# The last tile of a Winograd convolution in joint stages, and the place of a bound's product

## The chip, the cores and the metric

The kernel runs on one core of a Trainium2 chip. Its time is the device time of one launch in microseconds (us); lower is better. The core's engines are TensorE (PE; its weight loads are listed as PEld), VectorE (DVE), ScalarE (ACT), GpSimd (POOL) and SyncE (SP), which issues DMA transfers. Each engine works through its own instructions in order and waits on semaphores for the others.

## The reference

The input `x` is (4, 256, 48, 48) in float32. Two layers are applied, each to a group norm of `x` and with a residual.

```python
# layer 0
h = relu(batch_norm(conv3x3(gn(x))))                 # 256 -> 256 channels
q, k, v = split(qkv_w @ h + qkv_b)                   # 8 heads of 32
a = softmax(q^T k * 32 ** -0.5)
x = x + proj_w @ (v a^T) + proj_b
# layer 1
g = conv3x3(gn(x))                                   # 45 channels
outs = [gn(x)]
for i, d in enumerate((1, 6, 12, 24, 36)):
    w = softmax(g[:, 9 * i : 9 * i + 9])             # nine weights per pixel
    outs.append(sum of nine shifts of gn(x) by -d, 0, d, each times its weight)
y = conv1x1(concat(outs))
x = x + batch_norm(y)
```

## The kernel before

Channels lie on the 128 partitions in NH = 2 halves, pixels in the free dimension. The four images pass through two kinds of work: `attention` (layer 0's scores, exponentials and weighing), and the rest. From the second image on, the rest is done in three joint stages: `dynamic_filters` of image b - 1 (layer 1), and in the gaps of it `conv_qkv` of image b (conv, then q's, k's and v's products). The stages run at about 525 to 806, 1186 to 1469 and 1848 to 2107 us of the profiled span; each ends in the attention of image b. Image 0 has `conv_qkv` alone, to 150 us.

**The order of work.** Python writes one order of instructions for each engine. In a joint stage `drive` decides it. It holds several generators ("streams": `loads`, `far`, `rest`, `near`, `filters`, `mixes`) and one filler, `other`, which is `conv_qkv`. Each stream yields a due time; the first stream in the list that is due at the planner's time of TensorE goes next, and only if none is due the filler goes, when `need[0]()` is no later than that time. Otherwise the planner's TensorE time is moved to the soonest due time. The times are kept by `Clock`, one number per engine, raised by fixed prices (480 ns for a VectorE sum out of PSUM, 450 for a ScalarE copy and so on). They decide the order alone; the hardware then runs each engine's list in order.

`either` gives a sum of two SBUF tiles to VectorE or GpSimd, whichever the clocks say ends sooner (900 against 1300 ns for 576 elements, half of that for 288). `busy_dve` tells whether VectorE's clock is over 500 ns ahead of both ScalarE's and TensorE's.

**The conv in joint stages, `conv_blocks`.** It is a Winograd convolution in rows and columns. `Blocks` makes the transformed inputs (`stage0`, `rest`, `along`); the transformed weights are fetched by `taken`, two tiles ahead. There are twelve tiles, `TILES`: a row index i out of ORDER = (1, 2, 3, 4, 0, 5) and an output half o. A tile has four products, for the column indices j = 1, 2, 0, 3 (n = 0 to 3), each over the two input halves, into a PSUM tile of 128 x 288 out of a pool with two banks (tag "c", `psum_tile`; `free["c"]` and `slot("c", 2)` keep the planner's times of release). The column transform back is

- n = 0: ScalarE copies the product into `one` (L1190);
- n = 1: with a busy VectorE, ScalarE copies into `two[:, 1]` (L1195), and two `either` sums make `two[:, 0]` = one + product and `two[:, 1]` = one - product; else VectorE does both from PSUM (L1200, L1201);
- n = 2, 3: product + `two[:, 0]`, or `two[:, 1]` - product, into every second column of `y`: with a busy VectorE a ScalarE copy (L1206) and an `either` sum, else one VectorE sum out of PSUM (L1211, L1213).

The row transform back is in `before`, called within the first product, and `after`, called behind the fourth. For i = 1 to 4, `after` makes the sums and differences s12, d12, s34, d34 in `blocks.held`. For i = 5, `before` makes `t` = d12 - 2 d34, the result of row 1, and overwrites d12 with d12 - 8 d34, both by `axpy` on VectorE (L1073); `after` adds d12 to `y`, 576 elements, by `either` (L1102 on GpSimd, L1104 on VectorE), which is row 3. i = 0 goes likewise with rows 2 and 0. A finished row is put on a list by `relu`, and `relus(limit)` issues the ScalarE activations (L1125) that write the conv's output `hid`.

After the last tile, (5, 1), all open relus are issued, and the first product of q (L1255) is open to `drive` from their end on: `need[0]` holds `last[0]`.

**q, k and v, in `conv_qkv`.** q and k are made per chunk of 384 pixels: two products over the halves (L1255), a ScalarE activation that adds the bias (L1262), a VectorE maximum of the absolute values (L1267). v is made in nine steps, t = 0, 2, ..., 16, of two 128-pixel blocks each (L1277), copied by ScalarE to `vT` (L1284). Behind the first, VectorE makes `top` out of the maxima (L1288 to L1290). Behind the ninth, one product of 128 x 2 (L1293) and a VectorE copy (L1294) write `bound`, a bound of the scores, read at the kernel's end:

```python
            pb = psum_tile(f"pb_{b}")
            nc.tensor.matmul(pb[:, :NH], hmat, top[:, 0], start=True, stop=True)
            nc.vector.tensor_copy(bound[:, b, :], pb[:, :NH])
```

`psum_tile` is the same pool of two banks. In image 0 another small product of that pool follows (L2463), and then, as in the other images, the score products (L1331), whose PSUM tiles take over the banks of the pools before.

In the profile, `cv_k`, `cv_q` and `cv_v` are the tiles that hold transformed inputs, `y` and `held`; `pc` is the conv's PSUM tile, `pq` and `pv` those of q, k and of v, `pb` that of the bound. `prod` and `near` (L1828, L1834), `wb` (L1815), `far` (L1762, L1504, L1506), `amat` (L1736), `bmat` (L1724) and `py` (L1926, L1992) belong to the filters' streams.

Of the kernel before, what the change touches and what calls it, by code (L numbers as in the profile page):

```python
# [8 lines left out]
F32 = mybir.dt.float32  # L9
F32R = mybir.dt.float32r  # L10
AF = mybir.ActivationFunctionType
ALU = mybir.AluOpType
# [5 lines left out]
P = 128  # L18
NH = C // P
# [38 lines left out]
def conv_preact_kernel(  # L58
# [12 lines left out]
    nc = tc.nc  # L71
# [463 lines left out]
    hmat = const.tile([P, P], F32, tag="hmat", name="hmat")  # L535
# [5 lines left out]
    bound = const.tile([P, B, NH], F32, tag="bound", name="bound")  # L541
# [10 lines left out]
    with tc.tile_pool(name="w", bufs=1) as wpool, tc.tile_pool(  # L552
        name="act", bufs=1
# [59 lines left out]
        one = wpool.tile([P, 1], F32, tag="one", name="one")  # L613
# [20 lines left out]
        for j in range(2):  # L634
            t = act.tile([P, NH, PADW * PADW], F32, tag=f"pad{j}", name=f"pad{j}")
            t = t.rearrange("p h (r w) -> p h r w", w=PADW)
# [104 lines left out]
        clock = Clock()  # L741
        free = {}

        def slot(tag, bufs):

            ends = free.setdefault(tag, [])
            return ends[-bufs] if len(ends) >= bufs else 0.0
# [14 lines left out]
        XN = 2 * TJ * XT  # L762
        TILES = [(i, o) for i in ORDER for o in range(NH)]
# [334 lines left out]
        def either(out, a, c, op, *after):  # L1098

            part = 0.5 if len(out.shape) == 2 and out.shape[-1] == XN else 1.0  # L1100
            if clock.t["POOL"] + 1300 * part <= clock.alone(*after) + 900 * part:
                nc.gpsimd.tensor_tensor(out, a, c, op)  # L1102
                return clock("POOL", 1300 * part, *after)
            nc.vector.tensor_tensor(out, a, c, op)  # L1104
            return clock.both(900 * part, *after)

        def conv_blocks(b, psum_tile, blocks, pool, hid):

            axpy = blocks.axpy
            tt = nc.vector.tensor_tensor  # L1110
            rows = hid.rearrange("p h (t r w) -> p h t r w", r=4, w=WW)
            spare = list(blocks.spare)

            results, last = [], [0.0]

            def busy_dve():
                return clock.t["DVE"] > max(clock.t["ACT"], clock.t["PE"]) + 500

            def relu(o, r, y, end):
                results.append((o, r, y, end))  # L1120

            def relus(limit):
                while results and results[0][3] + 150 <= limit:
                    o, r, y, end = results.pop(0)
                    nc.scalar.activation(  # L1125
                        rows[:, o, :, r, :], rows_of(y), AF.Relu,
                        bias=bn_t[:, o : o + 1], scale=bn_s12[:, o : o + 1],
                    )
                    clock("ACT", 660, end)

            def before(i, o):

                s12, d12, s34, d34 = (blocks.held[:, j, o] for j in range(4))
                if i == 0:
                    t = spare.pop(0)
                    axpy(t, s34, -4.0, s12)
                    relu(o, 2, t, clock.both(800))
                    either(s12, s12, s34, ALU.subtract)
                elif i == 5:
                    t = spare.pop(0)  # L1140
                    axpy(t, d34, -2.0, d12)
                    relu(o, 1, t, clock.both(800))
                    axpy(d12, d34, -8.0, d12)
                    clock.both(800)

            def target(i, o):

                if i in (1, 3):
                    return blocks.first[o]
                if i in (2, 4):  # L1150
                    return blocks.held[:, 1 if i == 2 else 3, o]
                return spare.pop(0)

            def after(i, o, y):

                s12, d12, s34, d34 = (blocks.held[:, j, o] for j in range(4))
                if i in (2, 4):
                    s, d = (s12, d12) if i == 2 else (s34, d34)
                    either(s, y, blocks.first[o], ALU.add)
                    either(d, blocks.first[o], y, ALU.subtract)  # L1160
                elif i in (0, 5):
                    relu(o, i and 3, y, either(y, y, s12 if i == 0 else d12, ALU.add))

            blocks.scaled()
            need[0] = lambda: 150 + max(slot("c", 2), blocks.end[STEPS[0]])
            for t, (i, o) in enumerate(TILES):
                u = us.pop(t)
                y = target(i, o).rearrange("p (n s) -> p n s", s=2)
                for n, j in enumerate((1, 2, 0, 3)):
                    m = psum_tile(f"pc_{b}_{i}_{o}_{j}")[:, :XN]  # L1170
                    clock("PE", 0, slot("c", 2), blocks.end[i, j])
                    z = blocks.of[i].rearrange("p (j h n) -> p j h n", j=4, h=NH)[:, j]
                    relus(max(clock.t["ACT"], clock.t["PE"]))
                    for h in range(NH):
                        nc.tensor.matmul(
                            m, u[:, h, j], z[:, h], start=(h == 0), stop=(h == NH - 1)
                        )
                        clock("PE", MM * XN / CH)
                        if h == 0:
                            need[0] = lambda: 0.0  # L1180
                            if n == 0:
                                if t + 2 < len(TILES):
                                    us[t + 2] = taken(t + 2)
                                if t == 0:
                                    blocks.along(ORDER[1])
                                before(i, o)
                            yield MM * XN / CH
                    if n == 0:
                        one = pool.tile([P, XN], F32, tag="one", name=f"one_{b}_{i}_{o}")
                        nc.scalar.copy(one, m)  # L1190
                        end = clock("ACT", 400, clock.t["PE"])
                    elif n == 1:
                        two = pool.tile([P, 2, XN], F32, tag="two", name=f"two_{b}_{i}_{o}")
                        if busy_dve():
                            nc.scalar.copy(two[:, 1], m)  # L1195
                            end = clock("ACT", 400, clock.t["PE"])
                            either(two[:, 0], one, two[:, 1], ALU.add, end)
                            either(two[:, 1], one, two[:, 1], ALU.subtract, end)
                        else:
                            tt(two[:, 0], m, one, ALU.add)  # L1200
                            tt(two[:, 1], one, m, ALU.subtract)  # L1201
                            end = clock("DVE", 900, clock.t["PE"], end)
                    else:
                        to = y[:, :, n - 2]
                        if busy_dve():
                            nc.scalar.mul(to, m, 1.0 if j == 0 else -1.0)  # L1206
                            end = clock("ACT", 450, clock.t["PE"])
                            either(to, to, two[:, n - 2], ALU.add, end)
                        else:
                            if j == 0:  # L1210
                                tt(to, m, two[:, 0], ALU.add)  # L1211
                            else:
                                tt(to, two[:, 1], m, ALU.subtract)  # L1213
                            end = clock("DVE", 480, clock.t["PE"])
                        if n == 3:
                            after(i, o, y.rearrange("p n s -> p (n s)"))
                    free["c"].append(end)
                    then = STEPS[4 * t + n + 1] if 4 * t + n + 1 < len(STEPS) else None
                    need[0] = lambda: 150 + max(
                        slot("c", 2), blocks.end.get(then, NEVER) if then else last[0],  # L1220
                    )
                    if n == 3 and o == NH - 1:
                        blocks.passed.add(i)
                    if then is None:
                        relus(NEVER)
                        last[0] = clock.t["ACT"]
                    yield MM * XN / CH
# [4 lines left out]
        def conv_qkv(b, gn, psum_tile, weights, ready, pool, between=()):  # L1232
# [14 lines left out]
            top = small.tile([P, 2, NH], F32, tag="qktop", name=f"qktop_{b}")  # L1247
# [25 lines left out]
            for t in range(0, NT, 2):  # L1273
# [15 lines left out]
                    nc.vector.tensor_tensor(top[:, 0], top[:, 0], top[:, 1], ALU.mult)  # L1289
                    nc.vector.tensor_scalar(top[:, 0], top[:, 0], QS, None, ALU.mult)  # L1290
                yield 4 * MM * C / CH
            pb = psum_tile(f"pb_{b}")
            nc.tensor.matmul(pb[:, :NH], hmat, top[:, 0], start=True, stop=True)  # L1293
            nc.vector.tensor_copy(bound[:, b, :], pb[:, :NH])  # L1294

        qkv = {}
        CONV_QKV = MM * (6 * 4 * 6 * TN / CH + NCK * NH * 4 + NT * 2 * C / CH)
# [1354 lines left out]
```

## Time and profile before

| | us |
|---|---|
| median of three runs | 2724.35 |
| the runs | 2721.27, 2724.35, 2724.39 |
| profiled execution, its own time | 2722.09 |
| its span, first to last instruction | 2720.2 |

| engine | busy us | share of the span |
|---|---|---|
| TensorE, products | 2607.0 | 96% |
| TensorE, weight loads | 1102.1 | 41% |
| VectorE | 2082.2 | 77% |
| ScalarE | 1806.3 | 66% |
| GpSimd | 809.3 | 30% |

A busy share is a mean over stages of different kinds, so a change in one stage is read from that stage: which engine waits there, and for whom. The mean granted clock of TensorE is 0.989 of full speed, and a window of the trace can be asked for its own. In a timeline row the numbers are the start in the span and the length in us, then the engine, the line, the operation, the tiles and shapes, the count, and in brackets how long the engine stood idle before it and what ended that. Products in float32 show as two instructions each.

### The profile page before, as it was taken

Reading aid. Unit: us, or ns where it says so; the run is one execution under the profiler, and the core shown is the slowest. Engines: PE = TensorE matmul, PEld = TensorE weight load, DVE = VectorE, ACT = ScalarE, POOL = GpSimd, SP = SyncE. Lnnn points to the kernel's source line nnn. Section 1 sums busy time; section 2 is a strip of 40 time slices with the busy share of each in tenths; the row PEclk is TensorE's granted clock in tenths of the full one; section 3 lists DMA queues with packets and bytes.
Section 4 is the critical chain, followed back from the end, with each engine's and each line's share of the span. In section 5 each row is a group of like instructions: output and inputs, shape, how many; then the busy total and the mean of one; then the engine's idle time right before and its main releaser. Section 6 shows DMA issues by size and latency. Waiting matters only on the chain. (4 is left out here: it accounts for less than half of the span.)

```text
span 2720.2 us, 42536 instructions
## 1 busy us (share of the span) xinstructions
PE 2607.0 (96%) x16938; PEld 1102.1 (41%) x16938; DVE 2082.2 (77%) x2029; ACT 1806.3 (66%) x2287; POOL 809.3 (30%) x885
## 2 busy tenths in 40 slices
PE   6999999999999999999999999999989999999996
PEld 5632222555562222355555222245546222235554
DVE  7768888757739898857774988885775888885676
ACT  4479888734449898854445888884444888875344
POOL 5200100477520010067750000007775000100453
PEclk9999999999999999999999999999999999999998
DMA  4805445323252445423324354452324444432456
GB/s 174 223 13 105 108 98 110 90 60 108 65 104 58 99 95 108 99 74 87 94 63 84 76 105 99 94 111 75 84 73 120 107 100 99 99 88 72 121 165 219
DMA packets 136942, 273.67 MB, mean 101 GB/s; under 512 B 58024, under 2 KB 98384, under 8 KB 135712
## 3 DMA queue, kind: packets, MB, share of 16 engines
q0 software_dynamic: 26256, 137.71, 22.1%
q1 hardware_dynamic: 110480, 133.17, 18.3%
q8 instruction: 135, 2.21, 0.3%
q14 instruction: 71, 0.58, 0.1%
HBM read 112.12 MB, written 36.04 MB: 54 GB/s over the span
## 5 line engine op out<-in xcount | busy, mean ns | idle before, releaser
L1380 DVE TENSOR_TENSOR acc<-acc,p 128x2048 f32<-128x2048 f32 (+1 forms) x568 | 1052.0, 1852 | 121.0 <-ACT p L1340 71.6
L1340 ACT ACTIVATE p<-se 128x1536 f32<-128x1536 f32 x648 | 938.7, 1449 | 0.0
L1331 PE MATMUL so<-q,k 32*128 32x512 f32 (+1 forms) x1440 | 729.1, 594 | 18.5 <-ACT p L1339 15.9
L1331 PE MATMUL se<-q,k 32*128 32x512 f32 (+1 forms) x4320 | 737.8, 594 | 0.0
L1365 PE MATMUL num<-p,vT 128*32 128x512 f32 (+1 forms) x5760 | 711.9, 561 | 2.2 <-ACT ao L1390 2.2
L1339 ACT ACTIVATE p<-so 128x512 f32<-128x512 f32 x648 | 388.4, 599 | 195.2 <-PE se L1331 89.0
L1331 PEld LDWEIGHTS so<-q,k 32*128 32x128 f32 x1440 | 216.7, 183 | 535.6 <-ACT p L1339 492.0
L1834 POOL TENSOR_TENSOR near<-near,prod 128x384 f32<-128x384 f32 x352 | 353.3, 1037 | 255.3 <-DVE prod L1828 246.4
L1384 POOL DMA_DIRECT2D ring<-p x124 | 105.5, 851 | 776.4 <-ACT p L1340 481.4
L1365 PEld LDWEIGHTS num<-p,vT 128*32 128x32 f32 x5760 | 137.1, 108 | 480.2 <-issue 449.7
L1828 DVE TENSOR_TENSOR prod<-wb,pad 128x768 f32<-128x768 f32 x192 | 181.9, 953 | 84.6 <-ACT wb L1815 51.8
L1331 PEld LDWEIGHTS se<-q,k 32*128 32x128 f32 x4320 | 227.3, 183 | 5.1 <-ACT p L1340 4.1
L1815 ACT COPY wb<-ws 128x384 f32<-128x384 f32 x216 | 108.5, 506 | 166.0 <-DVE prod L1828 129.0
L1382 POOL DMA_DIRECT2D ring<-p x32 | 17.9, 559 | 632.2 <-ACT p L1340 485.1
L1992 PE MATMUL py<-far,wsc 128*128 128x384 f32 x512 | 169.9, 487 | 0.0
L1536 PE MATMUL pg<-pad,wcat 128*45 128x384 f32 x864 | 146.7, 490 | 8.5 <-ACT lg L1594 8.5
L1255 PE MATMUL pq<-hid,wqkv 128*128 128x384 f32 x384 | 133.1, 501 | 15.0 <-ACT hid L1125 12.8
L1504 ACT COPY far<-far 128x512 f32<-128x512 f32 x86 | 90.2, 1108 | 81.1 <-PE far L1762 77.8
L1992 PEld LDWEIGHTS py<-far,wsc 128*128 128x128 f32 x512 | 96.2, 190 | 66.0 <-issue 1.8
L1255 PEld LDWEIGHTS pq<-hid,wqkv 128*128 128x128 f32 x384 | 73.1, 194 | 69.2 <-ACT hid L1125 15.1
L1380 DVE TENSOR_TENSOR acc<-p,p 128x2048 f32<-128x2048 f32 x36 | 82.2, 2285 | 20.8 <-ACT p L1340 14.6
L1736 DVE COPY_PREDICATED amat<-along_y,bmat 128x768 f32<-128x768 uint32 x72 | 92.0, 1277 | 2.4
(334 smaller groups left out, 2865.1 us busy)
## 6 DMA issues: line engine op xcount, KB each, us to landing
ring<-p POOLq DMA_DIRECT2D x156, 768.0 KB, 5.7
ws<-w_d SPq DMA_DIRECT2D x216, 192.0 KB
ring<-u_d SPq DMA_DIRECT2D x36, 512.0 KB
pad<-in_x SPq DMA_DIRECT2D x14, 1152.0 KB
xst<-in_x POOLq DMA_DIRECT2D x36, 192.0 KB, 3.7
x_d<-pad SPq DMA_DIRECT2D x36, 192.0 KB
u_d<-pad SPq DMA_DIRECT2D x12, 512.0 KB
y_d<-y SPq DMA_DIRECT2D x13, 384.0 KB
```

The source lines that it names most:

```text
L1255: nc.tensor.matmul(pq[:, :CH], wqkv[:, i, s, g * P : (g + 1) * P], hid[:, i, cols], start=(i == 0), stop=(i == NH - 1),)
L1331: nc.tensor.matmul(dst[:, at : at + n], k_[r, g, m * P : (m + 1) * P], q[r, g, q0 : q0 + n], start=True, stop=True,)
L1339: nc.scalar.activation(p[:, 0, :], s1, AF.Exp, scale=QS)
L1340: nc.scalar.activation(p[:, 1:, :], s3, AF.Exp, scale=QS)
L1365: nc.tensor.matmul(st["num"][r, at : at + n], vT[:, m, g * P + j * D : g * P + (j + 1) * D], p[:, j, at : at + n], start=(m == 0 and not s ...
L1380: nc.vector.tensor_tensor(st["acc"][:, js], other[:, js], p[:, js], ALU.add)
L1384: nc.gpsimd.dma_start(out=extra, in_=p[:, 1:], accum_op=ALU.add)
L1536: nc.tensor.matmul(pg[64 * s : 64 * s + NG, :CH], wcat[:, ii, k, :], shifted(ii, cc, k // 3 - 1, k % 3 - 1), start=(i == 0 and k == 0), st ...
L1815: nc.scalar.copy(pw[:, :CH], fetched[c, k][0])
L1828: nc.vector.tensor_tensor(prod.rearrange("p h (r w) -> p h r w", w=WW), wb, src, ALU.mult)
L1834: nc.gpsimd.tensor_tensor(cat[:, h], cat[:, h], prod[:, h], ALU.add)
L1992: nc.tensor.matmul(py[c][:, o, :CH], wsc[:, n * NH + i, o * P : (o + 1) * P], rhs, start=(n == 0 and i == 0), stop=(n == order[-1] and i = ...
```

## The change

It has two parts. In the last tile of the conv, (5, 1), the row term d12 is added to the column terms ahead: behind the first product two VectorE sums of 288 elements make `two[:, 0]` and `two[:, 1]` out of `one` and every second column of d12. The second product is then added to the first of these and subtracted from the second in place: from a ScalarE copy by `either` with a busy VectorE, else by VectorE from PSUM. The third and fourth products give the finished row by one VectorE sum each, out of PSUM, whatever `busy_dve` says, and `after` adds nothing to this tile. Only that tile of the twelve is changed. Tiles (0, 0), (0, 1) and (5, 0) keep their row sum.

In `conv_qkv` of every image the bound's product and copy move from behind v's ninth step to behind its fifth (t = 8), and the planner is told of them.

```diff
             def before(i, o):
...
-                    either(s12, s12, s34, ALU.subtract)
-                elif i == 5:
+                    return s12, either(s12, s12, s34, ALU.subtract)
+                if i == 5:
...
                     axpy(d12, d34, -8.0, d12)
-                    clock.both(800)
+                    return d12, clock.both(800)
...
-            def after(i, o, y):
+            def after(i, o, y, end):
...
                 elif i in (0, 5):
-                    relu(o, i and 3, y, either(y, y, s12 if i == 0 else d12, ALU.add))
+                    if not TILES.index((i, o)) + 1 == len(TILES):
+                        end = either(y, y, s12 if i == 0 else d12, ALU.add)
+                    relu(o, i and 3, y, end)
...
-                                before(i, o)
+                                base = before(i, o)
                             yield MM * XN / CH
-                    if n == 0:
+                    if n == 0 and base and t + 1 == len(TILES):
+                        one = pool.tile([P, XN], F32, tag="one", name=f"one_{b}_{i}_{o}")
+                        nc.scalar.copy(one, m)
+                        end = clock("ACT", 400, clock.t["PE"])
+                        two = pool.tile([P, 2, XN], F32, tag="two", name=f"two_{b}_{i}_{o}")
+                        for s in range(2):
+                            tt(two[:, s], one, base[0][:, s::2], ALU.add)
+                        base = clock.both(960, base[1], end)
+                    elif n == 1 and base and t + 1 == len(TILES):
+                        if busy_dve():
+                            one = pool.tile([P, XN], F32, tag="one", name=f"uno_{b}_{i}_{o}")
+                            nc.scalar.copy(one, m)
+                            end = clock("ACT", 400, clock.t["PE"])
+                            either(two[:, 0], two[:, 0], one, ALU.add, end)
+                            either(two[:, 1], two[:, 1], one, ALU.subtract, end)
+                        else:
+                            tt(two[:, 0], m, two[:, 0], ALU.add)
+                            tt(two[:, 1], two[:, 1], m, ALU.subtract)
+                            end = clock("DVE", 900, clock.t["PE"], base)
+                    elif n == 0:
...
                         to = y[:, :, n - 2]
-                        if busy_dve():
+                        if busy_dve() and t + 1 < len(TILES):
...
-                        if n == 3:
-                            after(i, o, y.rearrange("p n s -> p (n s)"))
+                        if n == 2:
+                            first = formed
+                        else:
+                            after(i, o, y.rearrange("p n s -> p (n s)"), max(first, formed))
...
                 yield 4 * MM * C / CH
-            pb = psum_tile(f"pb_{b}")
-            nc.tensor.matmul(pb[:, :NH], hmat, top[:, 0], start=True, stop=True)
-            nc.vector.tensor_copy(bound[:, b, :], pb[:, :NH])
+                if t == 8:
+                    pb = psum_tile(f"pb_{b}")
+                    nc.tensor.matmul(pb[:, :NH], hmat, top[:, 0], start=True, stop=True)
+                    nc.vector.tensor_copy(bound[:, b, :], pb[:, :NH])
+                    free["c"].append(clock("DVE", 200, clock("PE", 100, slot("c", 2))))
```

`formed` is what the third and fourth branch set beside `end`: the planner's end of the sum.

More of the change, by code (lines that the diff above doesn't have):

```diff
@@ L1204, in conv_blocks @@
                         to = y[:, :, n - 2]
-                        if busy_dve():
+                        if busy_dve() and t + 1 < len(TILES):
                             nc.scalar.mul(to, m, 1.0 if j == 0 else -1.0)
                             end = clock("ACT", 450, clock.t["PE"])
-                            either(to, to, two[:, n - 2], ALU.add, end)
+                            formed = either(to, to, two[:, n - 2], ALU.add, end)
                         else:
@@ L1213, in conv_blocks @@
                                 tt(to, two[:, 1], m, ALU.subtract)
-                            end = clock("DVE", 480, clock.t["PE"])
-                        if n == 3:
-                            after(i, o, y.rearrange("p n s -> p (n s)"))
+                            end = formed = clock("DVE", 480, clock.t["PE"])
+                        if n == 2:
+                            first = formed
+                        else:
+                            after(i, o, y.rearrange("p n s -> p (n s)"), max(first, formed))
                     free["c"].append(end)
```

## The prediction

> **What bounds the kernel now.** The page first: TensorE is busy 96% of the span, VectorE 77%, so what counts is where TensorE stands still. In the list of costliest groups, the row of q's and k's products (L1255) carries one such wait:
>
> ```profile
> L1255 PE MATMUL pq<-hid,wqkv 128*128 128x384 f32 x384 | 133.1, 501 | 15.0 <-ACT hid L1125 12.8
> ```
>
> 12.8 us in front of 384 products, released by the relu (L1125) that writes the conv's output. The waits of TensorE, asked stage by stage, give it once per joint stage: 3.0, 3.0 and 6.1 us. It is the last TensorE wait of stages 1 and 2: from there to their ends (739.4 to 806.4 us, 1401.6 to 1468.7) no other is listed, so what is saved here arrives at the end. The third stage's row:
>
> ```profile
> PE pq L1255 <- ACT hid L1125: 6.1, 1, 6.1
> ```
>
> The timeline at the end of the first stage's conv (start, length, engine, line) shows the tail that the change attacks:
>
> ```profile
> 734.24 0.74 ACT L1206 ACTIVATE cv_q<-pc 128x288 f32<-128x288 f32 x2
> ...
> 735.30 1.62 DVE L1104 TENSOR_TENSOR cv_q<-cv_q,two 128x288 f32<-128x288 f32 x2
> ...
> 735.48 0.91 PE L1255 MATMUL pq<-hid,wqkv 128*128 128x384 f32 x2
> 735.53 2.24 POOL L1834 TENSOR_TENSOR near<-near,prod 128x384 f32<-128x384 f32 x2 [2.66 <-DVE prod L1828]
> 736.96 1.43 DVE L1104 TENSOR_TENSOR cv_q<-cv_q,cv_v 128x576 f32<-128x576 f32 x1
> ...
> 738.42 0.87 ACT L1125 ACTIVATE hid<-cv_q,bn_t_f,bn_s 128x576 f32<-128x576 f32 x1 [3.44 <-DVE cv_q L1104]
> ...
> 739.34 1.39 PE L1255 MATMUL pq<-hid,wqkv 128*128 128x384 f32 x2 [2.95 <-ACT hid L1125]
> ```
>
> Two copies out of PSUM, two sums, the row sum, the relu; then q's second half-product can start. The windows view of the time just after adds a second cost: the granted clock is 0.50.
>
> ```profile
> 739.65:743.06 3.41, 3.41 (x11) 1.58 (x10) 1.67 (x3) 1.83 (x4) 1.24 (x2) 0.50 0.14 54
> ```
>
> Two products and eight of far (L1762) take 1.39 and 2.08 us there, against 0.91 and 1.13 for the same groups earlier: 1.43 us lost. Stage 2 has the same rows (1400.67, 1401.59; clock 0.50 from 1401.83). In stage 3 the tail lies on GpSimd, beside VectorE's slowed work:
>
> ```profile
> 2026.10 1.33 DVE L1073 SCALAR_TENSOR_TENSOR cv_q<-cv_v 128x576 f32<-128x576 f32 x1
> 2026.78 2.60 POOL L1102 TENSOR_TENSOR cv_q<-cv_q,two 128x288 f32<-128x288 f32 x2
> 2027.47 1.25 DVE L1073 SCALAR_TENSOR_TENSOR cv_v<-cv_v 128x576 f32<-128x576 f32 x1
> ...
> 2029.46 1.40 POOL L1102 TENSOR_TENSOR cv_q<-cv_q,cv_v 128x576 f32<-128x576 f32 x1
> 2030.89 0.87 ACT L1125 ACTIVATE hid<-cv_q,bn_t_f,bn_s 128x576 f32<-128x576 f32 x1 [2.55 <-POOL cv_q L1102]
> ```
>
> For the bound, the timeline where conv_qkv of image 0 ends:
>
> ```profile
> 149.73 0.28 PE L1293 MATMUL pb<-qktop,hmat 128*128 128x2 f32 x2
> 149.93 0.59 ACT L1284 COPY vT<-pv 128x512 f32<-128x512 f32 x1 [1.14 <-PE pv L1277]
> 150.04 0.16 DVE L1294 COPY bound<-pb 128x2 f32<-128x2 f32 x1 [13.85 <-PE pb L1293]
> ...
> 150.26 1.05 PE L2463 MATMUL pb<-vbc,wp 128*128 128x1 f32 x8 [0.25 <-DVE bound L1294]
> ```
>
> v's last product ends at 149.89; the next user of a bank of this tag starts at 150.26, before the copy of v's last bank ends (150.52): it took the bound's bank.
>
> **What the Trainium skill says.** "TensorE: Matmul & The Clock Gate", What's actually happening: the clock is halved or restored by activity in free-running windows of 3413 ns. The trace agrees: the slow stretch is 3.41 us and follows 2.95 us of standstill. A wait of 2.33 us at 529.7 brought none, its twins at 1190 and 1852 did (0.50); so short waits are cheap and 2 to 3 us is a toss. "SBUF — State Buffer", Who interferes with whom: a VectorE instruction with two SBUF inputs contends with GpSimd reads, one with at most one SBUF input does not. The trace agrees: the 128x288 sum of two SBUF tiles takes 0.45 us alone (712.92) and 0.81 beside GpSimd (735.30), the sums with a PSUM input (L1211, L1213) 0.44 to 0.47 throughout.
>
> **The change part by part.**
> *Stages 1 and 2, ahead.* New at the tile's first product: two 128x288 VectorE sums of the copied product and every second row term, behind the two scaled sums (L1073) at 715.15 and 715.93; 0.45 us each by the row at 712.92 (bounds 0.44 and 0.81; an interleaved operand stands in L1104 already without a surcharge). At the second product, a copy by ScalarE as before and two sums in place. Before, the first went to GpSimd and the second to VectorE; `either` compares clocks, and VectorE's is now 0.96 ahead, so both go to GpSimd: 0.92 each, to about 719.2. Cover: the third and fourth products come 14 us later (732.76), behind py products that need none of this. Without the cover it would be 2.7 us. GpSimd's next sum (718.85) slips 0.4 us into an idle time of 4.4.
> *The tail.* Removed: two ScalarE copies (0.74), two sums beside GpSimd (1.62), the row sum (1.43). Added: two VectorE sums from PSUM, 0.45 each. VectorE's queue there holds a far copy to 733.99 and near's product 734.43 to 735.39, so the sums run to 736.2; the relu starts at 736.25, not 738.42, and q's half-product at 737.15, not 739.34: 2.2 us. Their banks are now freed by VectorE, the first at 735.8 against 734.6, and q's first half-product (735.48) starts at 735.85; it ends at 736.8, still inside the wait. TensorE then stands 0.8 us instead of 2.95, too little for a slow window by the trace's waits, so I add the 1.43: **3.6 us per stage, 7.2 for two**. Bounds: 1.5 (the slow window falls all the same, the sums queue behind one more 0.96 product) to 4.0.
> The planner's due time for q's first product falls by some 0.8 us; far's eight products, whose bank is free earlier, stay ahead of it. Nothing else is issued, no DMA is added, and no DMA is moved past another on SP's or POOL's queue.
> *Stage 3.* All four products run back to back here, so nothing covers the sums ahead. The three amat copies (L1736) take 5.17 us beside GpSimd, 3.12 alone; the scaled sums 1.3 beside it, 0.75 alone. GpSimd now idles until the row-term sums exist. VectorE: amat ends 0.8 earlier, 2025.4; scaled sums to 2026.9; row-term sums to 2027.8. GpSimd's two sums, 1.2 and 0.9, about 2027.3 to 2029.5; VectorE's last two wait for them and end at 2029.9; relu, q at 2030.8 against 2031.81. Gain **1.0**, from -2 (GpSimd at its 1.5 per sum, VectorE standing behind it) to +4 (a slow window fewer). The slow clock (0.50 from 2029.88 to 2036.7) I leave as it is.
> *Bound.* The same two products and 0.16 us copy, among v's products. The next v product takes the bound's bank, as the row at 150.26 does: 149.89 to 150.26 gives 0.37 us per image, at most 0.7 if it waits for v's copy (0.59). Behind the VectorE copy nothing stands for images 0 to 2 (VectorE waited 13.9 us there); in stage 3 near's products share the queue, up to 1 us more. Saved at the end: 0.37 for image 0; 0.1 each for images 1 and 2, where the score products wait for v's copy anyway (807.09); 0.1 for image 3, whose first score waited 1.99 us for the bound's copy (to 2107.46), but the statistics ahead of it read the same kind of bank until 2107.41. Net 4 x 0.37 - 0.67 = **+0.8** (0 to +3).
> *Sum.* -7.2 - 1.0 + 0.8 = -7.4 us. Against the profiled execution, 2722.09 (span 2720.2 and 1.9 around it): 2714.7. That execution lies 2.3 under the median of the runs, 2724.35, one other run as low; I take the middle, **2716.0**.
>
> **The rivals.**
> *A, the clock gives nothing* (0.24): standstill shrinks, but slow windows move elsewhere, and stage 3 gains nothing. 2 x 2.2 - 0.8 = 3.6 us: 2719.6. For it: whether 2.33 us slows the clock varied by stage. Against: 0.8 us never did.
> *B, GpSimd becomes stage 3's bound* (0.06): VectorE stands in order behind GpSimd sums of 1.5, q starts 2 us later, and the clock stays slow one window more (1.7): -7.2 + 3.7 + 0.8, 2720.5. For it: 1.47 mean in that row. Against: VectorE is free of contention meanwhile.
> *C, slower: the order moves* (0.12). The planner's clocks shift in all stages; TensorE is in order, and a product placed ahead of its operand costs a wait of 2.3 us and half of a 3.4 us window, as at 1190: about 4.0. Place: where far's and near's products are slotted among q's and v's. Two such places eat the gain; with four, -7.4 + 16 gives 2733. Against: after 739.4 and 1401.6 there is no wait, with 34 us of q and v products behind the last filter product.
> That the change doesn't shorten the tail at all would need the final sums to wait for GpSimd in stages 1 and 2, done 14 us before.
>
> **How the numbers follow.** The forecast has 0.58, its own range 2711 to 2718.5. A measurement tells about 0.2%, 5.4 us: faster means below 2718.9. A and B are within it, C is slower. Range 2711 to 2723: below, every gain at its upper end, 4 + 4 + 4; above, only C and A with a bound copy late in stage 3.
>
> **What would show it.** The wait of q's products on the relu at about 0.8, 0.8 and 5 us; no copy by ScalarE in the last two products and no 128x576 sum behind them; clock 1.00 just after in stages 1 and 2; both in-place sums on GpSimd; a gap of about 0.4 us behind v's fifth product pair. It is wrong if new TensorE waits appear among q's, far's and near's products, or v's products stand for the bound's copy.

## The result and the profile after

The changed kernel takes 2716.92 us (median of 20 runs, 2710.5 to 2729.62) against 2724.2 of the kernel before beside it (20 runs): a ratio of 0.9975, 95% interval 0.9966 to 0.9985, or 6.8 us less (4.1 to 9.3; the two medians lie 7.3 apart). The forecast was 2716.0.

The page of the changed kernel names the same bound, TensorE, with VectorE 5.4 us less busy and GpSimd 7.6:

```profile
PE 2608.3 (96%) x16938; PEld 1104.6 (41%) x16938; DVE 2076.8 (76%) x2033; ACT 1805.2 (66%) x2281; POOL 801.7 (30%) x884
```

In its costliest groups, the row of q's and k's products (L1255 before, L1278 now) carries 8.8 us of idle time instead of 15.0, and the main releaser is no longer the relu but the first of VectorE's two closing sums (L1232), which reads the third product and so frees its PSUM bank for q's first half-product:

```profile
L1278 PE MATMUL pq<-hid,wqkv 128*128 128x384 f32 x384 | 132.3, 499 | 8.8 <-DVE cv_q L1232 5.9 <-ACT q L1285 1.4 <-ACT hid L1125 0.7
```

The timeline at the end of stage 1's conv answers the one shown of before. The two sums follow each other straight out of PSUM, the relu follows them, and q's second half-product starts 0.35 us late instead of 2.95:

```profile
738.40 0.96 DVE L1853 TENSOR_TENSOR prod<-wb,pad 128x768 f32<-128x768 f32 x1 [0.44 <-ACT wb L1840]
739.27 0.45 DVE L1232 TENSOR_TENSOR cv_q<-pc,two 128x288 f32<-128x288 f32 x1
...
739.64 0.45 DVE L1234 TENSOR_TENSOR cv_q<-two,pc 128x288 f32<-128x288 f32 x1
739.78 0.91 PE L1278 MATMUL pq<-hid,wqkv 128*128 128x384 f32 x2 [0.26 <-DVE cv_q L1232]
740.12 0.87 ACT L1125 ACTIVATE hid<-cv_q,bn_t_f,bn_s 128x576 f32<-128x576 f32 x1 [1.82 <-DVE cv_q L1234]
741.04 0.91 PE L1278 MATMUL pq<-hid,wqkv 128*128 128x384 f32 x2 [0.35 <-ACT hid L1125]
```

In the windows view of the 3.4 us behind it, the column after POOL's count is the granted clock: 1.00, where before had 0.50. PE starts 14 instructions there instead of 11.

```profile
741.00:744.40 3.40, 3.36 (x14) 2.01 (x15) 2.07 (x4) 2.92 (x4) 1.36 (x2) 1.00 0.19 38
```

In stage 3, the row-term sums (L1196), GpSimd's two sums in place (L1102) and the two from PSUM form the tail. VectorE stands 0.68 and 0.29 us for GpSimd, and TensorE 5.42 for the first of the two closing sums (L1232), that is for a bank; the relu's end, at 2029.23, follows while q's first half-product runs at half clock:

```profile
2025.61 0.83 DVE L1196 TENSOR_TENSOR two<-one,cv_v 128x288 f32<-128x288 f32 x2
2026.21 1.63 POOL L1102 TENSOR_TENSOR two<-two,uno 128x288 f32<-128x288 f32 x2 [4.06 <-DVE two L1196]
2027.12 0.46 DVE L1232 TENSOR_TENSOR cv_q<-pc,two 128x288 f32<-128x288 f32 x1 [0.68 <-POOL two L1102]
...
2027.72 3.85 PE L1278 MATMUL pq<-hid,wqkv 128*128 128x384 f32 x5 [5.42 <-DVE cv_q L1232]
2027.87 0.46 DVE L1234 TENSOR_TENSOR cv_q<-two,pc 128x288 f32<-128x288 f32 x1 [0.29 <-POOL two L1102]
2028.36 0.87 ACT L1125 ACTIVATE hid<-cv_q,bn_t_f,bn_s 128x576 f32<-128x576 f32 x1 [2.75 <-DVE cv_q L1234]
```

The bound of image 0, now amid v's products, with the gap behind it (0.25 in the products' row, 0.34 in that of the weight loads):

```profile
143.51 0.28 PE L1317 MATMUL pb<-qktop,hmat 128*128 128x2 f32 x2
...
143.83 0.16 DVE L1318 COPY bound<-pb 128x2 f32<-128x2 f32 x1 [6.95 <-PE pb L1317]
144.04 6.77 PEld L1300 LDWEIGHTS pv<-wqkv,hid 128*128 128x128 f32 x32 [0.34 <-DVE bound L1318]
144.04 7.17 PE L1300 MATMUL pv<-wqkv,hid 128*128 128x256 f32 x32 [0.25 <-DVE bound L1318]
```

**Where the time went, segment by segment.** TensorE's instructions come in one order in both kernels, but for the bound's products, so the span can be cut at the same instructions. The table does this for one profiled execution of each kernel. `tail_alone` and `bound_alone` are described below.

| from, to | before | after | tail_alone | bound_alone |
|---|---|---|---|---|
| start to image 0's first score | 151.24 | 151.94 | 152.66 | 151.11 |
| last conv product to k's first, stage 1 | 8.59 | 5.01 | 5.01 | 8.65 |
| the same, stage 2 | 8.65 | 5.01 | 5.01 | 8.70 |
| the same, stage 3 | 9.66 | 8.82 | 8.82 | 9.66 |
| from there to v's first, stage 3 | 36.73 | 36.49 | 36.42 | 36.14 |
| v's first to first score, image 0 | 17.91 | 17.91 | 17.91 | 17.91 |
| v's first to first score, stage 1 | 15.75 | 16.27 | 15.75 | 16.27 |
| the same, stage 2 | 15.75 | 16.27 | 15.75 | 16.27 |
| the same, stage 3 | 37.58 | 38.16 | 37.22 | 38.16 |
| stage 1's conv, first to last product | 204.35 | 206.40 | 204.71 | 206.11 |

The tails give 3.58, 3.64 and 0.84. The bound costs nothing in image 0, 0.52 in each of stages 1 and 2, and 0.58 in stage 3. The sum is 3.58 + 3.64 + 0.84 - (0.52 + 0.52 + 0.58) = 6.4 us, near the 6.8 of the ratio and well inside its interval.

Two rows vary among kernels that are alike there, so their differences say nothing of the change. The row behind stage 3's tail is 36.73 before and 36.14 in bound_alone, with the same long tail (35.90 to 36.69 in three kernels of experiments 4 and 5). And with the bound in its old place, stage 3's way from v to the first score takes 37.2 to 37.6 us in six kernels, so that the bound's cost there is 0.6 to 0.9. The first row has a half-clock window in after and tail_alone, and none in before and bound_alone.

The two profiled spans differ by only 2.6 us, 2717.6 against 2720.2. Most of what is missing lies in stretches that the change doesn't touch, such as the last row. The experiments show how far such stretches vary.

### The profile page after: what moved, and what is told of

It reads as the page before. It is cut to its first block, busy times and chain, and to the rows that moved or that the text cites. A ratio compares the mean times of both kernels' runs of the same rounds, so it can differ in the third digit from the quotient of the medians.

```text
span 2717.6 us, 42542 instructions
## 1 busy us (share of the span) xinstructions
PE 2608.3 (96%) x16938; PEld 1104.6 (41%) x16938; DVE 2076.8 (76%) x2033; ACT 1805.2 (66%) x2281; POOL 801.7 (30%) x884
## 5 line engine op out<-in xcount | busy, mean ns | idle before, releaser
L1278 PE MATMUL pq<-hid,wqkv 128*128 128x384 f32 x384 | 132.3, 499 | 8.8 <-DVE cv_q L1232 5.9
L1278 PEld LDWEIGHTS pq<-hid,wqkv 128*128 128x128 f32 x384 | 72.8, 193 | 62.8 <-issue 8.5
```

The lines of the kernel that those rows point to most:

```text
L1278: nc.tensor.matmul(pq[:, :CH], wqkv[:, i, s, g * P : (g + 1) * P], hid[:, i, cols], start=(i == 0), stop=(i == NH - 1),)
```

## The experiments

Each kernel is timed beside the kernel before; "under" is the ratio's difference from 1 in us. The median of before isn't the same each time (2723.25, 2722.65, 2723.77), so kernels of different experiments are compared by their ratios. Segments are from one profiled execution of each kernel. None of the kernels leaves out work.

**1. The two halves.** `tail_alone` leaves the bound in its old place, `bound_alone` moves only the bound.

```diff
-                if t == 8:
-                    pb = psum_tile(f"pb_{b}")
...
+            pb = psum_tile(f"pb_{b}")
```

> The last tile's change alone; the bound's product stays behind v's ninth step. My theory (the tail gives the whole gain and the bound's move costs some): the wait for the relu at q's products stays at 0.6 us in stages 1 and 2, clock 1.00 behind it, 3.6 us less from the last conv products to the k products in each, some 0.8 in stage 3; without the bound's move v's nine steps run without a gap. 8.0 us under the kernel before in all, so about 1 us less than with both parts. Rival (the bound's move helps too, since its product and copy no longer stand in front of the first scores): 1 us more than with both parts, or 6 under the kernel before.

> The bound's move alone; the last tile as before. My theory: each image pays a gap of 0.3 to 0.6 us behind v's fifth step (TensorE waits for the bound's or v's copy) and gets back 0.2 to 0.4 at the first scores: 0 to 1.1 us slower than before, not to be told from it. Rival (gain of the bound): 1 us or more faster, the wait of 2.0 us of the first score of the last image gone.

tail_alone: 2713.52 (7 runs), ratio 0.9966 (0.9954 to 0.9978), 9.3 us under. bound_alone: 2723.97 (13 runs), 1.0000 (0.999 to 1.001). So the tail is the whole gain. The table's columns show that each half does in the whole what it does alone. That the bound costs about 1.6 us is read from segments; the times (9.3 under without it, 6.8 with it) agree, but their intervals overlap.

**2. The in-place sums on VectorE.** The changed kernel, with these sums on VectorE in all three stages; stage 3 is the one without cover.

```diff
-                            either(two[:, 0], two[:, 0], one, ALU.add, end)
-                            either(two[:, 1], two[:, 1], one, ALU.subtract, end)
+                            tt(two[:, 0], two[:, 0], one, ALU.add)
+                            tt(two[:, 1], two[:, 1], one, ALU.subtract)
+                            clock.both(900, end)
```

> The changed kernel, with the two in-place sums of the second product always on VectorE instead of GpSimd. My theory: in stages 1 and 2 nothing, since they have 14 us of cover. In stage 3 the two sums take 0.45 each behind the row-term sums instead of 0.8 each on GpSimd and two hand-overs, and VectorE no longer stands for GpSimd: q's first half-product starts 0.8 us earlier than in the changed kernel. In all 0.5 to 1 us under the changed kernel. Rival (GpSimd's help is worth it, VectorE is the bound in the tail): 0.5 us over it.

2716.05 (8 runs), 0.997 (0.9959 to 0.998): not to be told from the change itself. Stage 3's segment from the last conv product to k's first takes 8.46 instead of 8.82, less than half of what was expected. The segment behind it takes 36.83 instead of 36.49, so that nothing is left of this (the slow window lies across both). TensorE still waits for the first of the two closing sums:

```profile
2021.56 0.45 DVE L1204 TENSOR_TENSOR two<-two,uno 128x288 f32<-128x288 f32 x1
2021.93 0.45 DVE L1233 TENSOR_TENSOR cv_q<-pc,two 128x288 f32<-128x288 f32 x1
...
2022.53 8.73 PE L1279 MATMUL pq<-hid,wqkv 128*128 128x384 f32 x17 [5.36 <-DVE cv_q L1233]
```

In this kernel's timeline no wait of VectorE is listed from 2012.66, where its predicated copies begin (bmat, then amat for 4.70 us), to the last sum. So VectorE's own queue sets this tail, and GpSimd's part is 0.36 us. Rival B, with q 2 us later in stage 3, didn't come: q comes 0.84 earlier.

**3. The bound in a bank of its own.** The changed kernel, with the bound's product in a PSUM pool that v's products don't use:

```diff
-                    pb = psum_tile(f"pb_{b}")
+                    pb = ps_m.tile([P, 512], F32, tag="misc", name=f"pb_{b}")
...
-                    free["c"].append(clock("DVE", 200, clock("PE", 100, slot("c", 2))))
+                    clock("DVE", 200, clock("PE", 100))
```

> The changed kernel with the bound's product in a bank that v's products do not use (the filters' bank, idle there). My theory (the bound's price is the wait of v's next product for its bank): no gap behind v's fifth step but the 0.2 us of the product itself; v's nine steps and the first scores 0.3 us shorter per image, 1 us under the changed kernel. Rival (the move itself costs nothing and the difference between both parts and the tail alone was chance): no difference from the changed kernel.

2715.5 (11 runs), 0.9967 (0.9955 to 0.998). The segments from v's first product to the first score fall from 16.27, 16.27 and 38.16 to 15.86, 15.86 and 37.44; before had 15.75, 15.75 and 37.58. The rows of v's products among the costliest groups of the changed kernel and of this one tell why: the waits for the bound and for v's copy are gone.

```profile
L1300 PE MATMUL pv<-wqkv,hid 128*128 128x256 f32 x288 | 65.2, 382 | 1.6 <-DVE bound L1318 0.8 <-ACT vT L1307 0.6 <-DVE gstd_n L97 0.3
```

```profile
L1300 PE MATMUL pv<-wqkv,hid 128*128 128x256 f32 x288 | 65.0, 382 | 0.3 <-DVE gstd_n L97 0.3
```

Image 0's falls from 17.91 to 17.50. So the bound's price is mainly that of the bank it shares, as the prediction had it: 1.9 us (0.41 in each of images 0 to 2, 0.72 in the last). In the time alone this isn't seen, since the intervals of the two kernels overlap.

**4. How much of the tail is clock?** `fill_before` is the kernel before, with idle products (identity by a resident weight, 256 columns, results unused) ahead of q's first product: TensorE computes while it would stand. `fill_12` has them in stages 1 and 2 alone; `fill_one` is a control with one per stage.

```diff
+            if b and c == g == s == 0:
+                fill = ps_m.tile([P, 512], F32, tag="misc", name=f"fill_{b}")
+                busy(fill, (0, 5, 5, 11)[b])     # fill_12: 5, 5, 0; fill_one: 1, 1, 1
             pq = psum_tile(...)
```

> The kernel before, with products that compute nothing of use (identity times a weight, into a bank of PSUM that is free there) ahead of q's first product: 5, 5 and 11 in stages 1, 2 and 3. It leaves the tail and the relu where they are and only keeps TensorE occupied while it waits. My theory (the slow stretch behind the wait comes from the standstill): clock 1.00 after the relu, 1.4 us less in stages 1 and 2 and about 2.4 in stage 3, 5 us under the kernel before in all, although q's first full product starts no earlier. Rival (the slow stretch has another cause, or the time is lost elsewhere): no difference.

> The kernel before, with idle products ahead of q's first product in stages 1 and 2 alone (5 each), none in stage 3. Filling all three took 15 us off, of which its profile shows 1.3, 1.4 and about 1 behind the three waits, the rest in stretches that the filling does not touch: fewer windows of half clock, and one attention 5 us shorter. My theory (the rest is where the windows happen to fall, a product of few runs): 3 us under the kernel before, from -8 to 0. Rival (filling itself does something more, wherever it stands): 8 to 10 us under it.

> A control: the kernel before with one idle product (0.5 us) ahead of q's first product in each stage, so the same tile and the same order, but TensorE stands still for 2.5 of the 2.95 us and 5.6 of the 6.1. Theory that standstill sets the slow clock: at most 1 us under the kernel before. Rival (the extra tile and instructions themselves, by their place in memory or by the bank, bring the 15 us): 8 us or more under it.

In stages 1 and 2 the expectation for fill_before holds. The clock behind the relu is full, and the segment takes 7.28: 1.31 and 1.37 us are the clock's, and the remaining 2.27 down to the changed kernel's 5.01 are the standstill's. TensorE now waits 0.80 us for the relu, and far's eight products take 1.24 us instead of 2.08:

```profile
736.87 2.43 PE L1305 MATMUL fill<-wsc,ident 128*128 128x256 f32 x10
...
740.74 0.91 PE L1258 MATMUL pq<-hid,wqkv 128*128 128x384 f32 x2 [0.80 <-ACT hid L1125]
...
741.58 1.24 PE L1765 MATMUL far<-amat,xT 64*128 64x256 f32 x8
```

In stage 3 it doesn't hold. The eleven products end too early (4.91 us long), TensorE still stands 2.44 us for the relu, and one slow window of 3.41 us follows instead of 6.83. The two segments behind the conv fall by 0.7 us in sum, where 2.4 was expected. In fill_one TensorE stands 2.53 us, a slow window follows in stages 1 and 2 as in before, and the segment takes 8.77 and 8.76.

The totals fit worse: 2707.93 (5 runs), 0.9944 (0.993 to 0.9957), 15 us under where 5 were expected; fill_12 2710.99 (6 runs), 0.9947 (0.9927 to 0.9967), 14 under where 3 were; fill_one 2720.54 (22 runs), 0.9991 (0.9983 to 0.9999), 2.5 under where at most 1 was. Kernels that keep the long tail are as fast as the changed kernel or faster. Of the 14 to 15 us, between 11 and 12 aren't in these segments.

**5. Is it the wait that is filled, or the added instructions?** `shift_only` puts the same five idle products into stages 1 and 2 of the kernel before, ahead of v's first step, where nothing waits.

```diff
+                if b in (1, 2) and t == 0:
+                    busy(ps_m.tile([P, 512], F32, tag="misc", name=f"fill_{b}"), 5)
                 pv = psum_tile(...)
```

> The kernel before, with the same 5 idle products in stages 1 and 2 as the filled version had, but ahead of v's first step, where TensorE does not wait: they cost their own 2.4 us twice, and leave the tails as they were. Filling the two waits took 12 us off, of which 3 lie behind the waits; the units of the attentions that follow differ in the same way in both filled versions. Theory A (more instructions on TensorE's list move what comes after them, and some of the 12 us is that): 2 to 6 us under the kernel before in spite of the added work. Theory B (the 12 us come from the filled waits, through the clock, in ways that one profile does not show): 5 us over it.

2719.5 (22 runs), 0.9984 (0.9975 to 0.9992): 4.4 us faster, although its own segments from k's first product to v's first grow by 2.3 and 2.0 us (48.05 and 47.99 to 50.31 and 50.03), and the tails and the slow windows behind them stay (8.48 and 8.75). That can't be the filled wait. The largest difference is in stage 2's attention. From the first score to the next conv's first product it takes, in the profiled executions:

| idle products ahead of it, in stages 1 and 2 | us |
|---|---|
| none: before, bound_alone, vector_sums | 383.43, 383.13, 383.29 |
| none: after, tail_alone, own_bank | 382.17, 381.99, 381.62 |
| none: combo, combo2 of experiment 6 | 380.43, 380.60 |
| one each: fill_one | 379.44 |
| five each: fill_before, fill_12, shift_only, combo_shift | 378.41, 378.40, 378.21, 378.38 |

(before and vector_sums hold a half-clock window there, half of whose 3.41 us, 1.7, is lost if TensorE has work all through; in the others TensorE's clock was halved for 0.4 us at most.) Four different kernels with the same ten extra products agree within 0.2 us. Stage 1's attention, behind five of these products, shows no such step: 382.61, 382.52, 382.95 and 380.54 us in these four, 382.31 to 384.89 without. What can be seen is that TensorE's score products wait less for ScalarE's exponentials. From the waits of TensorE in this attention, total, times and longest in us; first before, then shift_only, then fill_before:

```profile
PE so L1331 <- ACT p L1339: 4.5, 5, 1.8
```

```profile
PE so L1333 <- ACT p L1341: 1.3, 5, 0.5
```

```profile
PE so L1334 <- ACT p L1342: 1.0, 3, 0.5
```

VectorE, ScalarE and GpSimd have the same instruction lists in these three kernels. Why ten more products on TensorE, five of them 20 to 70 us earlier and five one stage earlier, bring its products and the exponentials into better step isn't settled. Their position in the instruction stream is one candidate, a lasting shift between the two engines another; neither was isolated.

**6. The parts together.** `combo` is the changed kernel with experiments 2 and 3, ten idle products ahead of q's first in stage 3, and four ahead of the last image's first score. `combo2` takes the latter's bank from another pool; `combo_shift` is combo2 with the five idle products in stages 1 and 2. The cut shows the number of idle products against fill_before's line.

```diff
-                busy(fill, (0, 5, 5, 11)[b])
+                busy(fill, (0, 0, 0, 10)[b])     # combo_shift: 0, 5, 5, 10
...
+        if b == B - 1:
+            busy(three("ready")[:, 0], 4)        # combo2, combo_shift: a tile of tag "num"
```

> A version that should beat both: the changed kernel with the second product's in-place sums on VectorE, the bound's product in a bank that v does not use, 10 idle products ahead of q's first product in stage 3, and 4 ahead of the last image's first scores, where TensorE stands 2.1 us and then runs 6.8 us at half clock. My theory: 7 us of the change, 0.5 to 1 of the VectorE sums, 1 of the bound's bank, 1 to 2.4 of the filling in stage 3, 2 to 3.4 of the last scores: 12 to 15 us under the kernel before. Rival (windows of half clock only move): 8.

> As the version that joined all parts, but the 4 idle products ahead of the last image's first scores go into a bank that is free there; in that version they waited for the statistics themselves and held the scores up by 1.9 us. My theory: the first scores follow the statistics at once, with the clock at 1.00; 2 us under that version, 15 to 16 under the kernel before. Rival (the half clock falls there all the same): 1 us over that version.

> The same with 5 idle products ahead of q's first product in stages 1 and 2 too, where the change has left a wait of only 0.6 us: they cost 1.8 us each stage that nothing hides. Theory A (instructions added on TensorE's list shorten the attentions that follow): 2 to 6 us under the version without them. Theory B: 3.6 us over it.

combo: 2708.73 (6 runs), 0.9948 (0.9927 to 0.9968). In stage 3 the clock stays full, and the two segments behind the conv are 7.74 and 35.01 against 8.82 and 36.49 of the changed kernel:

```profile
2012.95 4.48 PE L1331 MATMUL fill<-wsc,ident 128*128 128x256 f32 x20
...
2018.53 0.88 PE L1282 MATMUL pq<-hid,wqkv 128*128 128x384 f32 x2 [1.10 <-DVE cv_q L1233]
...
2019.70 12.52 PE L1282 MATMUL pq<-hid,wqkv 128*128 128x384 f32 x38 [0.29 <-ACT hid L1125]
```

That is 2.56 us, and 2.54 less than with experiment 2 alone (8.46 and 36.83): the slow clock that the prediction left in stage 3 was worth some 2.5. The four products ahead of the last scores had a price: they wait for the statistics as the scores did, and hold the first score up by their own length:

```profile
2092.90 1.97 PE L1331 MATMUL ready<-wsc,ident 128*128 128x256 f32 x8 [2.11 <-DVE yst L1896]
```

combo2 was meant to mend that and did not. Its products wait 2.11 us for the same statistics, and stage 3's way from v to the first score is 39.34 us in both, against 37.44 in own_bank. It takes 2712.41 (7 runs), 0.9964 (0.995 to 0.9977), where 15 to 16 under was expected. combo_shift: 2710.09 (6 runs), 0.9954 (0.9938 to 0.997). Its five idle products have at most the 0.6 us of wait left to fill, lengthen those segments by 1.1 us each (5.00 and 5.01 to 6.11) and still lose nothing; but the intervals of the two overlap, so this only leans to experiment 5's reading. fill_before's interval lies below that of the changed kernel (0.9966 to 0.9985), combo's touches it, and the two can't be told from each other.

## Why the prediction was right

**Stages 1 and 2** were forecast at 3.6 us each and measured 3.58 and 3.64. Both terms hold: 2.2 of standstill is 2.27 by experiment 4, and 1.43 of slow clock is 1.31 and 1.37. The waits that remain, forecast at 0.8, came as two, 0.26 for the bank that VectorE's first sum frees and 0.35 for the relu; no window of clock 0.50 follows them in stages 1 and 2 of after, tail_alone, vector_sums, own_bank, combo and combo2, twelve cases. Behind 2.95 us (before, bound_alone, shift_only) one followed in all six.

The reason given was too simple, though. "Too little for a slow window by the trace's waits" and "0.8 us never did" don't hold for the whole trace of before. There is a place where TensorE's only wait of note is 0.68 us, and the clock is halved just behind (0.51 in the row below):

```profile
1887.85 0.87 PE L1714 MATMUL wT<-ident,wq 36*64 36x36 f32 x12 [0.68 <-DMA wq<-w_d]
```

```profile
1889.90:1893.30 3.40, 3.40 (x9) 2.39 (x8) 3.30 (x4) 1.82 (x3) 1.66 (x2) 0.51 0.42 139
```

So the length of the wait alone doesn't decide. That a window's activity decides is as the Trainium skill has it ("TensorE: Matmul & The Clock Gate", What's actually happening: free-running windows of 3413 ns), and within each execution the slow windows do start on one grid of that step (in before, 739.64, 1190.20 and 1401.83 us are 132 and 62 steps apart). The same section puts the slow clock behind an idle window of about 3.4 us; here, where less sufficed, the measurement decides. What sets the place of the 0.68 us apart from the tail wasn't tested; to that extent the 1.43 us rested on luck. Rival A, under which the clock gives nothing, falls for these stages.

**Stage 3** was forecast at 1.0 and measured 0.84. Its path held: the scaled sums took 0.75 each, the row-term sums 0.83 in all, both in-place sums went to GpSimd. Two sizes were off and made up for each other: amat became 0.45 us shorter (5.17 to 4.72) where 0.8 was forecast, and GpSimd's sums took 1.63 together instead of 2.1. The wait of q is 5.4, forecast at 5, but for a bank, not for the relu as the prediction had it. The slow clock of 6.8 us stayed, as said.

**The bound** was forecast at +0.8 (0 to +3); the segments give about +1.6. Experiment 3 measures the gap alone: 0.41 us in images 0 to 2, where 0.37 was forecast. In image 0 as much is saved at the end, as forecast. Two terms were mis-sized. In stage 3 it is 0.72, because v's next product there waits for v's copy (0.56), the case that the prediction named as the upper end. And the saving at the end, "0.1 each for images 1 and 2", is a loss of 0.11: even without the gap, 15.86 against 15.75. With or without the bound's product ahead, the second group of scores waits for the copy of v's last bank; in the timelines of stage 1, before and after, the weight load stands 0.34 and 0.45 us for it:

```profile
807.09 0.31 PEld L1331 LDWEIGHTS se<-q,k 32*128 32x128 f32 x6 [0.34 <-ACT vT L1284]
```

```profile
807.94 0.19 PEld L1356 LDWEIGHTS se<-q,k 32*128 32x128 f32 x3 [0.45 <-ACT vT L1307]
```

So the bound's product had stood in time that TensorE would have waited, and had cost next to nothing there. One sign that the prediction named for being wrong, v's products standing for the bound's copy, is at odds with its own path: they do stand for it, 0.25 us, within the gap that it forecast. The last image's score waits 2.11 us for the statistics instead of 1.99 for the bound: the statistics hold it, as said, and the 0.1 us forecast as saved isn't seen in this wait:

```profile
2105.37 1.19 PE L1356 MATMUL so<-q,k 32*128 32x512 f32 x1 [2.11 <-DVE yst L1890]
```

**Rival C**, an order that costs, didn't come: TensorE's instructions kept their order, but for the bound. What looks like it in the profiled execution of after, slow windows at 531.8, 569.4 and 654.7 us where before has none, is in fill_before, fill_12 and shift_only too, at least at the first place (532.3, 533.3, 535.4), and these have before's own instructions up to stage 1's tail. With those same instructions stage 1's conv took 204.35, 203.61, 205.68, 207.36 and 204.98 us (before, fill_before, fill_12, shift_only, fill_one), so its 206.40 in after needs no cause in the change. (The prediction counted this rival's 2733 from the median of the runs, the other forecasts from the middle between it and the profiled execution; counted alike it is 2732.)

The forecast's change was -7.4 us. The segments give -6.4, the tails 8.1 where 8.2 was forecast and the bound 1.6 where 0.8 was. That the medians lie 7.3 apart, and the measured one within a us of the forecast, is closer than the sum deserves. And shifts of attention time like experiment 5's, up to 5 us in one attention, could have hidden the gain: the forecast had no term for them.

## What to carry to other kernels

Of a chain of small operations between the last product and the next stage's first one, everything that doesn't need that product can be done ahead, under products that don't need it: here two copies, two sums and a row sum became two sums from PSUM, and the halved clock behind the wait went with them, more than a third of what stages 1 and 2 gained. A moved product takes its bank along: ask who gets the bank next, and whether the old place cost anything. An edit of 0.2% is below what one pair of profiles can show; cut the traces at the same instructions, and compare the untouched segments too before reading the total.

## What was not expected of the hardware

- Idle products were followed by a faster attention. With five each in stages 1 and 2, stage 2's took 378.2 to 378.4 us, in nine kernels without them or with one 379.4 to 383.4, the other engines' instructions being the same in before, fill_before, fill_12, shift_only and fill_one. Stage 1's attention showed no such step. The cause is open.
- Slow windows last 3.41 us, or two or three times as long, and their starts, taken modulo this length, differ from one execution to the next, while within one execution all starts leave the same remainder. Whether a given short wait meets one can so differ between executions. The total time at half clock in a profiled execution went from 34 us (combo) over 61 (before) to 68 (after); single runs of one kernel spread over 5 to 19 us.
- A wait of 2.3 us, TensorE's at the first conv product of a stage, brought a slow window in some executions and none in others; the 2.95 us ahead of q's second half-product (before, bound_alone, shift_only) were followed by one every time. Waits of 0.6 to 0.8 us at this place never were, but 0.68 us at another was.
